# A two-layer decoder on one core: jobs of a step in a fixed order, other steps for the first cross attention's jobs, input rounding on GpSimd

## The chip, the cores and the metric

The kernel runs on one core of a Trainium2 chip. The metric is the device time of one execution in microseconds (us); the time of a kernel is the median of its runs. Engines in the profile: PE is TensorE's matmuls, PEld its weight loads, DVE is VectorE, ACT is ScalarE, POOL is GpSimd, SP is the engine that issues most DMAs.

## The reference, cut to what matters

The input `x` is 16 samples of 128 tokens by 256 features, with a context of the same shape. Two layers follow; each block adds its result to `x` and normalises the rows (mean and variance over the 256 features).

```
x = layernorm(x + ternary_attention(x))      # 2 x 256 causal, 16 heads of 16
x = layernorm(x + rope_cross(x, ctx))        # per sample, 16 heads of 8 channels, 256 x 256
x = layernorm(x + top2_of_8_experts(x))
x = layernorm(x + latent_attention(x))       # causal, 16 heads, keys from a 64-wide latent
x = layernorm(x + cross(x, ctx, ctx))        # 8 heads of 16 channels
x = layernorm(x + gated_mlp(x) + product_key_experts(x))

# every projection of the ternary attention:
sx = 127 / clip(max(abs(x), axis=-1), 1e-5);  xq = round(x * sx) / sx
y  = xq @ wq.T                               # wq in {-1, 0, 1}, scaled
```

The causal attentions work on the samples as the kernel holds them, 128 tokens by 256 features, in 16 heads.

## The kernel before

The 16 samples lie in SBUF as 16 tiles `x_t[b]` of 128 by 256. The kernel runs the ternary attention and the first cross attention in one list of beats, then the experts (rows scattered to DRAM by expert, gathered again afterwards), then the latent attention and the second cross attention in a second list of beats, then the last block.

**Beats.** `by_beats` lays out a list of blocks. A block has H beats for each sample (2 in the causal attentions, 8 in the first cross attention, 4 in the second). In beat n TensorE makes two sets of scores: those of unit n as queries by keys, whose row maxima VectorE takes (`nm`, a TENSOR_REDUCE over 128 x 1024 in PSUM tile `ps_st`), and those of unit n - lag as keys by queries, with the maxima already subtracted by a small matmul (`nmT,pick`), which ScalarE turns into exponentials (`pT`). Then come the sums of unit n - lag - 2 (`ps_o<-pT,v`, and `ps_o<-pT,ones` for the denominators). After the sums come the jobs: small pieces of work for a sample i, each with an offset, done in beat `H*i + offset` of its block.

**What fixes the order.** Inside the beats every instruction of TensorE, VectorE, ScalarE and GpSimd is kept in the order in which it is written (`tc.keep_in_program_order`). So the order of the jobs of a beat is the order on each engine. Before, the jobs of a beat stand by block, then by sample (the older sample, whose offset is larger, first), then by the block's list. In the ternary attention this gives (m is the sample whose scores are being made):

| beat | order before |
|---|---|
| even, 2m | scale_rows (m-5), out_integers (m-4), divide (m-3), maxima (m-1), project (m+1), quantise (m+2) |
| odd, 2m+1 | finish (m-4), turn (m-3), parts (m), step (m+2) |

The jobs of the ternary attention: `quantise` finds the row maxima of a sample (`am`), their scale (`isx_x`, `sx`), rounds (`qround`, `qint_x`) and makes a diagonal of the scales (`diag`, `sv`). `step` turns the integers with TensorE (`ps_m<-identb,qint_x`, copied to `qT_x` by ScalarE) and makes a row of the scales with a matmul (`ps_m<-diag,ones`). `project` makes queries, keys and values (`qk`, `v`). `parts` splits the score maxima in three bf16 parts (five small VectorE instructions that write `nmx`), `maxima` turns them (`nmT`). `divide` takes the sums by their denominators (`r` by two activations, then `oT`). `turn` turns that back to rows and rounds it like an input (`am`, `isx_o`, `sx`, `qround`, `qint_o`, from PSUM), `out_integers` turns the integers, `finish` makes the output product, adds `x` (`xn`) and takes the row statistics (`st`, `mv`, `ve`, and `rstd` on GpSimd), `scale_rows` writes `x_t[b]`.

**PSUM.** All jobs share the tiles named `ps_m`. Up to beat 45 of the first list there are three of them, used strictly in turn; from there on there is one, and the score tiles `ps_st` are three instead of two. A new tile waits until all readers of the tile that held its place are done.

**The first cross attention.** H is 8 and the lag 11. Each sample has in addition `keys` and `queries` (rotations with VectorE, ScalarE and GpSimd, and four `z` multiplications on GpSimd), `values`, `out` (ScalarE copies the sums, `ol`), `spread`, `invert` (two activations on `l`), `divide` (`l<-ol,l` on VectorE), `finish`, `scale_rows`, and the gate of the experts: `gate_turn`, and for each pair of samples, at the odd one, `gate` (logits, two exponentials), `gate_best` (top two), `gate_rows`, `places` (row numbers in the experts' buffers) and four `scatter` DMAs from GpSimd's queue.

**GpSimd's start.** Ahead of the branch that holds the attentions GpSimd clears tiles and issues the loads of the context and of the weights of the later blocks, the last being `fkeys`.

Of the kernel before, what the change touches and what calls it, by code (L numbers as in the profile page):

```python
# [14 lines left out]
ALU = mybir.AluOpType  # L15
# [8 lines left out]
ROUND = 12582912.0  # L24
# [5 lines left out]
def kernel(ctx: ExitStack, tc: tile.TileContext, a: dict, out: bass.AP):  # L30
# [17 lines left out]
    x_t = []  # L48
# [53 lines left out]
    ident = const.tile([P, P], F32, name="ident")  # L102
# [99 lines left out]
    vec, act, pool = Written(nc.vector), Written(nc.scalar), Written(nc.gpsimd)  # L202
# [35 lines left out]
    def turned(out, src, identity):  # L238
        tc.keep_in_program_order(nc.tensor.transpose(out, src, identity))
# [30 lines left out]
    def by_beats(blocks, switch=None, at=None):  # L270

        begin, beats = 0, {}
        for H, lag, score, jobs, order in blocks:
            for i, b in enumerate(order):
                for h in range(H):
                    n = begin + H * i + h  # L280
                    beats.setdefault(n, [[], [], []])[0].append((score["beat"], (b, h), 0))
                    beats.setdefault(n + lag, [[], [], []])[0].append((score["beat"], (b, h), 1))
                    beats.setdefault(n + lag + 2, [[], [], []])[1].append((score["sums"], b, h))
                for off, job in jobs:
                    if callable(off):
                        off = off(i)
                    beats.setdefault(begin + H * i + off, [[], [], []])[2].append((job, b, i))
            begin += H * len(order)
        for n in sorted(beats):
            if n == at:  # L290
                switch()
            scores, sums, jobs = beats[n]
            for f in dict.fromkeys(f for f, _, _ in scores):
                on = {which: unit for g, unit, which in scores if g is f}
                f(on.get(0), on.get(1))
            for f, b, h in sums:
                f(b, h)
            for job, b, i in jobs:
                job(b)

    def own_columns(t, hd):
# [328 lines left out]
    wmean = const.tile([P, 4], F32, name="wmean")  # L630
# [7 lines left out]
    for w in range(4):  # L638
        t = pw0.tile([P, 2, D], F32, name="wround", bufs=2)
# [42 lines left out]
    def ternary(pl):  # L682


        def quantised(src, tag):

            am = small.tile([P, 1], F32, name="am")
            vec.tensor_reduce(am, src, AX.X, ALU.max, apply_absolute_value=True)
            isx = small.tile([P, 1], F32, name=f"isx_{tag}")
            vec.tensor_scalar(isx, am, EPS, 1.0 / 127.0, ALU.max, ALU.mult)  # L690
            sx = small.tile([P, 1], F32, name="sx")
            vec.reciprocal(sx, isx)
            t = pl["w"].tile([P, D], F32, name="qround")
            vec.tensor_scalar(t, src, sx, ROUND, ALU.mult, ALU.add)
            qb = pl["w"].tile([P, D], BF16, name=f"qint_{tag}")
            vec.tensor_scalar(qb, t, ROUND, None, ALU.subtract)
            return qb, isx

        def turned_integers(qb, tag):
# [7 lines left out]
        kept = {}  # L707

        def tail(last, others):

            return lambda i: last if i >= B - 2 else others

        def quantise(b):
            qb, isx = quantised(x_t[b], "x")

            diag = pl["w"].tile([P, P], F32, name="diag")
            vec.tensor_scalar_mul(diag, ident, isx)
            sv = small.tile([P, 1], F32, name="sv")
            vec.tensor_mul(sv, isx, wmean[:, 2:3])
            kept[b] = qb, diag, sv  # L720

        def step(b):
# [42 lines left out]
        def turn(b):  # L765

            ot = pl["m"].tile([P, 2, P], F32, name="ps_m")
            for c in range(2):
                turned(ot[:, c, :], kept[b][:, c, :], ident)
            kept[b] = quantised(ot.rearrange("p c d -> p (c d)"), "o")  # L770

        def out_integers(b):
            qb, iso = kept[b]
# [13 lines left out]
        def scale_rows(b):  # L787
            xn, stats = kept.pop(b)
            scaled(x_t[b], xn, stats)

        jobs = [(6, divide), (1, parts), (2, maxima), (tail(8, 7), turn), (tail(11, 8), out_integers),
                (tail(14, 9), finish), (tail(15, 10), scale_rows), (-2, project), (-3, step), (-4, quantise)]
        return 2, 3, causal_scores(pl, kept, qk_scale), jobs, range(B)


# [91 lines left out]
    def scatter(c, n):  # L887
        pool.indirect_dma_start(
            out=xs[:, :], out_offset=bass.IndirectOffsetOnAxis(ap=place[:, c, n : n + 1], axis=0), in_=x_t[c],
            in_offset=None,  # L890
        )
# [10 lines left out]
    def rope_cross_plain(pl):  # L902

        kept = {}
# [62 lines left out]
        def scale_rows(b):  # L967
            xn, stats = kept.pop(b)
            scaled(x_t[b], xn, stats)

        jobs = [(20, out), (21, spread), (22, invert), (23, divide), (8, parts), (9, maxima), (-11, biases), (-10, keys),
                (-5, queries), (5, values), (24, finish), (25, scale_rows)]
        for beat, part in ((26, gate_turn), (28, gate), (29, gate_best), (30, gate_rows), (31, places)):
            jobs.append((beat, lambda b, part=part: part(pl, b)))

        for k in range(4):
            jobs.append((33 + 2 * k, lambda b, k=k: b % 2 and scatter(b - 1 + k // 2, k % 2)))
        return 8, 11, cross_scores(pl, 16, kept, 11), jobs, range(B)

    def rope_cross_masked(st):  # L980
# [31 lines left out]
    with tc.If(taken_out == 0) as cmp:  # L1012
        with ExitStack() as st:
            pl, switch = attention_tiles(st, 4)
            ordered[0] = True
            by_beats([ternary(pl), rope_cross_plain(pl)], switch, 2 * B + 13)
            ordered[0] = False
    with cmp.Else():
        with ExitStack() as st:
            by_beats([ternary(attention_tiles(st, 4)[0])])  # L1020
        with ExitStack() as st:
            rope_cross_masked(st)
# [126 lines left out]
    sv = early.tile([P, NR, 2, 2, 8], F32, name="sv")  # L1149
    al = early.tile([P, NR, 2, 8, 8], F32, name="al")  # L1150
    sc = early.tile([P, NR, 2, 8], F32, name="sc")
    with ExitStack() as st:
# [7 lines left out]
        kept = {}  # L1160
# [89 lines left out]
        def scale_rows(b):  # L1250
# [2 lines left out]

        latent_block = (
            2, 3, causal_scores(pl, kept),
            [(6, divide), (1, parts), (2, maxima), (7, finish), (8, scale_rows), (-2, operands), (-3, latent_keys),
             (-4, scale_latent), (-5, latent), (-6, latent_turn), (-7, scale_combined), (-8, combine),
             (lambda i: -10 - min(i, 4), fetch)], range(B),
        )
# [60 lines left out]
        def score(hf, b):  # L1320
            R = b - NR
            if R < 0:
                return
            ps = pl["m"].tile([P, 2, 64], F32, name="ps_m")
            rows = slice(hf * 64, hf * 64 + 64)
            for t in range(2):
                mm(ps[:, t, :], lhsT=routes[R][rows, t, :], rhs=fkeys[rows, t, :], start=True, stop=True)
            act.copy(rt[:, R, hf], ps)

        def best(b):  # L1330
# [10 lines left out]
            for hf in range(2):  # L1341
# [1 line left out]

        cross_block = (
            4, 6, cross_scores(pl, 8, kept1, 6),
            [(11, cross_out), (12, cross_invert), (13, cross_add), (14, cross_scale), (4, cross_parts), (5, cross_maxima),
             (0, values), (-2, queries), (18, turn_block), (19, route), (23, lambda b: score(0, b)),
             (24, lambda b: score(1, b)), (25, best)],
            [b for R in range(NR) for b in (R, NR + R)],
# [305 lines left out]
```

## Time and profile before

| | |
|---|---|
| median of 3 runs | 1509.57 us (1507.97 to 1511.66) |
| profiled execution | 1506.95 us |
| its span, first to last instruction | 1505.2 us |
| mean granted TensorE clock | 0.962 |
| PE / DVE / ACT / POOL busy | 1363.2 / 808.6 / 600.3 / 292.0 us |

Where the stages lie in the span: first scores at 27.57 us, ternary attention to about 182, first cross attention to about 535, the passage to the experts to 565, latent attention from about 893 and second cross attention from about 1040 to 1240, last block to the end.

How to read a timeline row: start in us, duration in us, engine, line of the kernel, operation, output<-inputs by the program's names, shape, count; in brackets the idle time of the engine just before it and what ended that. L195 is the helper that records VectorE, ScalarE and GpSimd instructions of the beats and L236 and L239 record TensorE's, so the rows are told apart by their tiles.

### The profile page before, as it was taken

The page shows a single profiled execution, that of the slowest core. Times are in us where ns is not written, and L with a number is a line of the kernel's source. Part 1 is how long each engine was busy: PE and PEld are TensorE (multiplying, and loading weights), DVE is VectorE, ACT ScalarE, POOL GpSimd, SP SyncE. Part 2 cuts the span into 40 slices and gives each one's busy share as a digit, 9 for nine tenths or more (in the row PEclk, how much of TensorE's full clock was granted, in tenths as well). Part 3 has the DMA queues.
Part 4 walks back from the last instruction along what each step waited for, and adds up shares of the span by engine and source line. Part 5 has one row for each costly group of instructions (what it writes and reads, how often), then busy time and mean ns, then how long its engine had stood idle before and what let it go on. Part 6 is the DMA issues. An engine that isn't in the chain of part 4 may idle for free. (4 is left out here: it accounts for less than half of the span.)

```text
span 1505.2 us, 28639 instructions
## 1 busy us (share of the span) xinstructions
PE 1363.2 (91%) x12013; PEld 860.6 (57%) x12013; DVE 808.6 (54%) x2075; ACT 600.3 (40%) x1051; POOL 292.0 (19%) x404
## 2 busy tenths in 40 slices
PE   3999899999999939999999949999999998999997
PEld 2666555555555416777777636666555544446666
DVE  6899877777777520111111047886676756543322
ACT  1544435555555522111111124554455555771110
POOL 7000233443444120000000053311122110000000
PEclk9999989999999968999999959999999998999998
DMA  9200000000000016322221041100000000000000
GB/s 309 72 2 2 2 2 2 12 12 15 12 12 15 15 35 202 98 93 93 95 92 34 20 164 33 30 2 2 2 2 2 2 2 1 1 0 12 18 7 21
DMA packets 41744, 58.16 MB, mean 39 GB/s; under 512 B 4752, under 2 KB 31392, under 8 KB 41472
## 3 DMA queue, kind: packets, MB, share of 16 engines
q1 hardware_dynamic: 35984, 41.95, 8.6%
q0 software_dynamic: 4784, 13.42, 2.7%
q8 instruction: 99, 1.62, 0.5%
q10 hardware_dynamic: 832, 0.79, 0.2%
q14 instruction: 45, 0.37, 0.1%
HBM read 39.38 MB, written 16.78 MB: 37 GB/s over the span
## 5 line engine op out<-in xcount | busy, mean ns | idle before, releaser
L195 DVE TENSOR_REDUCE nm<-ps_st 128x4 f32<-128x1024 f32 (+1 forms) x256 | 312.9, 1223 | 136.7 <-PE ps_st L236 135.3
L195 ACT ACTIVATE pT<-ps_st 128x1024 f32<-128x1024 f32 x224 | 229.4, 1024 | 206.1 <-PE ps_st L236 205.4
L195 POOL TENSOR_TENSOR rstd<-ve,nhalf 128x1 f32<-128x1 f32 x112 | 62.9, 561 | 720.0 <-DVE ve L195 555.2
L236 PE MATMUL ps_o<-pT,v 128*32 128x256 f32 (+1 forms) x2560 | 164.7, 347 | 4.2 <-ACT ol L195 3.3
L1071 DVE TENSOR_TENSOR ye<-ps_e,b 128x256 f32<-128x256 f32 x40 | 17.0, 425 | 265.1 <-PE ps_e L1068 265.1
L236 PE MATMUL ps_st<-rot,z 32*128 32x256 f32 x1024 | 147.9, 406 | 1.4 <-DVE nm L195 1.4
L1060 ACT ACTIVATE h<-ps_h,b 128x640 f32<-128x640 f32 x64 | 50.8, 794 | 228.6 <-PE ps_h L1056 228.6
L1056 PE MATMUL ps_h<-h,w 128*128 128x320 f32 x512 | 139.1, 432 | 0.0
L236 PE MATMUL ps_st<-z,rot 32*128 32x512 f32 x512 | 131.7, 592 | 0.0
L1056 PEld LDWEIGHTS ps_h<-h,w 128*128 128x128 f32 x512 | 97.3, 190 | 40.5
L236 PEld LDWEIGHTS ps_o<-pT,v 128*32 128x32 f32 x2560 | 54.8, 108 | 101.3 <-issue 81.3
L236 PE MATMUL ps_st<-nmT,pick 32*128 32x256 bf16 x1024 | 100.6, 274 | 10.3 <-ACT nmT L195 7.7
L236 PEld LDWEIGHTS ps_st<-rot,z 32*128 32x128 f32 x1024 | 90.1, 187 | 13.0 <-issue 3.4
L195 POOL DMA_INDIRECT y<-ys,place x32 | 31.1, 971 | 312.3 <-DMA ys<-ye 304.6
L236 PE MATMUL ps_o<-pT,ones 128*32 128x256 f32 x1024 | 79.4, 381 | 0.0
L236 PEld LDWEIGHTS <-pick 32*128 32x128 bf16 x1024 | 30.6, 92 | 79.6 <-issue 72.9
L1056 PE MATMUL ps_h<-xeT,w 128*128 128x320 f32 x256 | 72.9, 443 | 2.3 <-DVE xeT L1046 1.1
L236 PE MATMUL ps_st<-ctx,z 32*128 32x256 f32 x512 | 73.0, 402 | 0.0
L1068 PE MATMUL ps_e<-w,h 128*128 128x256 f32 x320 | 70.4, 379 | 0.0
L236 PE MATMUL ps_f<-fxT,fgw 128*128 128x512 f32 x128 | 62.7, 613 | 6.7 <-ACT g L1373 6.7
L236 PE MATMUL ps_st<-z,ctx 32*128 32x512 f32 x256 | 66.6, 596 | 0.0
L1068 PEld LDWEIGHTS ps_e<-w,h 128*128 128x128 f32 x320 | 60.8, 190 | 9.1
(281 smaller groups left out, 2354.8 us busy)
## 6 DMA issues: line engine op xcount, KB each, us to landing
w<-in_W_dram SPq DMA_DIRECT2D x16, 512.0 KB, 4.0
w<-in_W_dram SPq DMA_DIRECT2D x8, 1024.0 KB, 5.3
xs<-zero SPq DMA_DIRECT2D x40, 128.0 KB, 4.5
xe<-xs SPq DMA_DIRECT2D x40, 128.0 KB, 3.8
ys<-ye SPq DMA_DIRECT2D x40, 128.0 KB, 2.1
x<-in_x_dram SPq DMA_DIRECT2D x16, 128.0 KB, 6.3
ctx<-in_ctx_dram POOLq DMA_DIRECT2D x16, 128.0 KB, 5.3
out_dram<-x SPq DMA_DIRECT2D x16, 128.0 KB, 1.7
```

Source lines behind the costliest of these rows:

```text
L195: instruction = getattr(self.engine, name)(*args, **kw)
L236: tc.keep_in_program_order(nc.tensor.matmul(*args, **kw))
L1056: nc.tensor.matmul(ps[:, n, 0:H], lhsT=w[:, c, hc * P : (hc + 1) * P], rhs=src[:, c, n * H : (n + 1) * H], start=(c == 0), stop=(c == part ...
L1060: nc.scalar.activation(dst[:, hc, :].rearrange("p (n t) -> p n t", n=2), ps[:, :, 0:H], AF.Gelu, bias=b12[:, layer, e, hc : hc + 1],)
L1068: nc.tensor.matmul(ps, lhsT=h2[:, fc, c * P : (c + 1) * P], rhs=w3[:, fc, :], start=(fc == 0), stop=(fc == 3))
L1071: nc.vector.tensor_add(ye[:, c, :], ps, b3[:, e, :])
```

## The change

Three things change. First, the jobs of a beat are sorted by block, then by their place in the block's list, then by sample; and the lists are written so that `parts` and `maxima` stand first. The jobs of the ternary attention then stand so:

| beat | order after |
|---|---|
| even, 2m | maxima (m-1), divide (m-3), out_integers (m-4), scale_rows (m-5), project (m+1) |
| odd, 2m+1 | parts (m), turn (m-3), finish (m-4), step (m+2), quantise (m+3) |

Second, in the first cross attention `divide`, `finish` and `scale_rows` move two beats later, the gate's jobs two to eight beats later and the scatters eight beats later. Third, the input's `quantise` does its two rounding instructions, the diagonal and `sv` on GpSimd instead of VectorE, and stands one beat earlier (-5 for -4). `turn`, which reads PSUM, still rounds on VectorE.

```diff
@@ by_beats
-                for off, job in jobs:
+                for k, (off, job) in enumerate(jobs):
                     if callable(off):
                         off = off(i)
-                    beats.setdefault(begin + H * i + off, [[], [], []])[2].append((job, b, i))
+                    beats.setdefault(begin + H * i + off, [[], [], []])[2].append((begin, k, i, job, b))
...
-            for job, b, i in jobs:
+            for _, _, _, job, b in sorted(jobs, key=lambda j: j[:3]):
                 job(b)
@@ ternary
-        def quantised(src, tag):
+        def quantised(src, tag, eng):
...
-            vec.tensor_scalar(t, src, sx, ROUND, ALU.mult, ALU.add)
+            eng.tensor_scalar(t, src, sx, ROUND, ALU.mult, ALU.add)
             qb = pl["w"].tile([P, D], BF16, name=f"qint_{tag}")
-            vec.tensor_scalar(qb, t, ROUND, None, ALU.subtract)
+            eng.tensor_scalar(qb, t, ROUND, None, ALU.subtract)
...
-            qb, isx = quantised(x_t[b], "x")
+            qb, isx = quantised(x_t[b], "x", pool)
...
-            vec.tensor_scalar_mul(diag, ident, isx)
+            pool.tensor_scalar_mul(diag, ident, isx)
...
-            vec.tensor_mul(sv, isx, wmean[:, 2:3])
+            pool.tensor_mul(sv, isx, wmean[:, 2:3])
...
-            kept[b] = quantised(ot.rearrange("p c d -> p (c d)"), "o")
+            kept[b] = quantised(ot.rearrange("p c d -> p (c d)"), "o", vec)
...
-        jobs = [(6, divide), (1, parts), (2, maxima), (tail(8, 7), turn), (tail(11, 8), out_integers),
-                (tail(14, 9), finish), (tail(15, 10), scale_rows), (-2, project), (-3, step), (-4, quantise)]
+        jobs = [(1, parts), (2, maxima), (6, divide), (tail(8, 7), turn), (tail(11, 8), out_integers),
+                (tail(14, 9), finish), (tail(15, 10), scale_rows), (-2, project), (-3, step), (-5, quantise)]
@@ rope_cross_plain
-        jobs = [(20, out), (21, spread), (22, invert), (23, divide), (8, parts), (9, maxima), (-11, biases), (-10, keys),
-                (-5, queries), (5, values), (24, finish), (25, scale_rows)]
-        for beat, part in ((26, gate_turn), (28, gate), (29, gate_best), (30, gate_rows), (31, places)):
+        jobs = [(8, parts), (9, maxima), (20, out), (21, spread), (22, invert), (25, divide), (-11, biases), (-10, keys),
+                (-5, queries), (5, values), (26, finish), (27, scale_rows)]
+        for beat, part in ((28, gate_turn), (32, gate), (33, gate_best), (35, gate_rows), (39, places)):
...
-            jobs.append((33 + 2 * k, lambda b, k=k: b % 2 and scatter(b - 1 + k // 2, k % 2)))
+            jobs.append((41 + 2 * k, lambda b, k=k: b % 2 and scatter(b - 1 + k // 2, k % 2)))
@@ latent_block
-            [(6, divide), (1, parts), (2, maxima), (7, finish), (8, scale_rows), (-2, operands), (-3, latent_keys),
+            [(1, parts), (2, maxima), (6, divide), (7, finish), (8, scale_rows), (-2, operands), (-3, latent_keys),
@@ cross_block
-            [(11, cross_out), (12, cross_invert), (13, cross_add), (14, cross_scale), (4, cross_parts), (5, cross_maxima),
+            [(4, cross_parts), (5, cross_maxima), (11, cross_out), (12, cross_invert), (13, cross_add), (14, cross_scale),
              (0, values), (-2, queries), (18, turn_block), (19, route), (23, lambda b: score(0, b)),
```

## The prediction, made before the changed kernel was run

> **What bounds the kernel now.** I read the busy shares first, then busy times by stage, then the timelines of one period of each attention, then the waits, and last the first 40 us engine by engine.
>
> ```profile
> PE 1363.2 (91%) x12013; PEld 860.6 (57%) x12013; DVE 808.6 (54%) x2075; ACT 600.3 (40%) x1051; POOL 292.0 (19%) x404
> ```
>
> The same by stage (start:end, length, busy PE, PEld, DVE, ACT, POOL, clock):
>
> ```profile
> 60.00:148.00 88.00, 79.14 (x1265) 53.58 (x1263) 82.00 (x256) 43.43 (x85) 6.41 (x11) 1.00 0.01 2
> 212.00:535.00 323.00, 307.13 (x3290) 169.43 (x3290) 226.38 (x484) 183.86 (x284) 122.15 (x147) 1.00 0.03 12
> ```
>
> The whole says TensorE; the stages differ. In the ternary attention (60 to 148 us) VectorE is busy 82.00 of 88 and TensorE 79.14; in the first cross attention (212 to 535) TensorE is idle 323 - 307.13 = 15.9 us. VectorE in one ternary period (O: odd beat, E: even beat):
>
> ```profile
> 102.39 1.22 DVE L195 TENSOR_REDUCE nm<-ps_st 128x8 f32<-128x1024 f32 x1
> 103.52 0.48 DVE L195 SCALAR_TENSOR_TENSOR xn<-ps_m,so,x 128x256 f32<-128x256 f32 x1
> ...
> 105.62 0.48 DVE L195 TENSOR_SCALAR qround<-ps_m,sx 128x256 f32<-128x256 f32 x1
> ...
> 107.26 1.22 DVE L195 TENSOR_REDUCE nm<-ps_st 128x8 f32<-128x1024 f32 x1
> ...
> 111.95 1.22 DVE L195 TENSOR_REDUCE nm<-ps_st 128x8 f32<-128x1024 f32 x1
> ```
>
> 102.39 to 111.95 is 9.56 us, with no wait over 0.1 us: VectorE sets this period. TensorE waits in it once, for a PSUM tile:
>
> ```profile
> 152.77 0.49 PE L236 MATMUL ps_m<-diag,ones 128*128 128x128 f32 x2 [1.03 <-DVE xn L195]
> 154.97 0.45 PE L236 MATMUL ps_m<-x,xw 128*128 128x256 f32 x1 [1.71 <-DVE qround L195]
> ```
>
> `ps_m` has three tiles in rotation here. The tiles before these two are, in order, the output product (read by `xn`), the turned output (read last by `qround`), the turned integers, the row of scales. So each tile waits for the reader of the third tile before it. That rule prices the new order. The start:
>
> ```profile
> 21.27 0.35 DVE L195 TENSOR_SCALAR qround<-x,sx 128x256 f32<-128x256 f32 x1
> 22.01 0.40 PE L239 MATMUL ps_m<-identb,qint_x 128*128 128x128 bf16 x2 [2.51 <-DMA xs<-zero]
> 26.72 0.40 PE L239 MATMUL ps_m<-identb,qint_x 128*128 128x128 bf16 x2 [1.94 <-DVE qint_x L195]
> 35.21 0.61 POOL L180 DMA_DIRECT2D fkeys<-in_f_keys_dram  x1 [3.42 <-DMA b<-in_b_dram]
> 35.98 0.60 POOL L180 DMA_DIRECT2D fkeys<-in_f_keys_dram  x1 [0.16 <-issue]
> ```
>
> GpSimd issues the loads of the context and the later weights until 36.58 us. They stand ahead of the branch into the attentions, so nothing inside the branch runs on GpSimd earlier. VectorE rounds the first sample at 21.27 and TensorE starts at 22.01.
>
> **Part 1, rounding on GpSimd: the start.** `qround`, `qint_x`, `diag` and `sv` leave VectorE. On GpSimd no such operation is in the trace on these operands; the nearest is
>
> ```profile
> L195 POOL TENSOR_SCALAR z<-rot,hm 128x256 f32<-128x256 f32 x64 | 58.1, 922 | 1.6
> ```
>
> 0.92 us for the same shape, and `rstd` on 128x1 takes 0.56. I take 0.92 each for `qround` and `qint_x` and 0.56 each for the two small ones, 2.96 a sample; the lower bound is VectorE's own 0.35 + 0.29. First transpose: 36.58 + 1.84 = 38.4 instead of 22.01, 16.4 late. Two things come back: the second transpose no longer waits for VectorE behind `qk` (1.94 us; GpSimd has the second `qint_x` at 36.58 + 2.96 + 1.84 = 41.4, TensorE could take it at 38.4 + 2.8 = 41.2), so 1.8; and a wait of 0.46 for `nmx` at 37.13, since parts come first. **+14**, from +12.5 (GpSimd at VectorE's price) to +16.4 (nothing comes back).
>
> **Part 2, the ternary loop.** Off VectorE go, start to start, 0.39 + 0.21 + 0.20 + 0.07 = 0.87 a period, 9.57 to 8.7. TensorE without waits needs 9.57 - 1.03 = 8.54. But the odd beat's order is now parts, turn, finish, step: the tiles go turned output, output product, turned integers, row of scales. So the row of scales waits for `qround` of the turned output, and VectorE reaches that only after `nm`, five parts instructions and four more. From the scores ready in O: `nm` 1.26, parts 0.92 (106.34 to 107.26), `am` 0.45, `isx` 0.19, `sx` 0.20, `qround` 0.48, hand-over 0.05: 3.55. Then the row of scales to the scores of E ready, 104.05 to 106.64: 2.59. E to O, with TensorE never waiting, 106.64 to 111.00: 4.36; VectorE's and ScalarE's E work fits in it (`nmT` first, then the two for `r` end 2.3 after, `oT`, `so`, `x`, `qk` end at 4.2). GpSimd's work hides: 2.96 and the 0.56 of `rstd`, which stands ahead of it in the beat, fit in one period, and `quantise` is now two beats ahead of `step`, not one. Period 3.55 + 2.59 + 4.36 = **10.50**, longer than the 9.57 although VectorE does less. TensorE stands 1.97 us in the wait instead of 1.03. It happens where turn and step share a beat: beats 7 to 27, eleven times. Beats 9 to 27 took 60.88 to 147.87, 9.67 each, nine of them: 9 x 0.83 = 7.5; beat 7 had no finish and its period was 8.15: +2.35; in beat 27 the 1.71 wait shrinks: -0.4. **+9.4**, from -8 (no such wait: VectorE's remaining 8.77 sets the period) to +12. Queued behind the wait on TensorE are all scores of the next beat, and `nm` and `pT` wait for those.
>
> Does GpSimd slow VectorE? `x` took 0.40 us without and 0.54 with GpSimd elementwise work beside it, `qint_o` 0.29 and 0.48 (at 190.99). Only `x` lies beside the new work; 0.14 in E, where 0.1 is spare: nothing. The Trainium skill (SBUF — State Buffer, "Who interferes with whom") speaks against this move: it calls the port pair that the two engines share an exclusive lock. By that, `x` could stand a whole 0.92 us, which would add 0.8 to each of 11 periods, some 9 us; the rows show 0.14.
>
> **Part 3, the passage to the cross attention.** Waits of 0.64 (`nmx`, 176.26) and 0.59 (`oT`, 184.79) go, since parts and divide come earlier. At 197.2 the clock fell to half for 10.24 us after a wait of 1.36; VectorE's load there is the same, so I leave it. **-1**, from -6 (no half clock, 5.1 back) to +5 (twice).
>
> **Part 4, the first cross attention.**
>
> ```profile
> PE ps_m L239 <- DVE nmx L195: 9.7, 14, 0.7
> PE ps_o L236 <- ACT ol L195: 3.3, 7, 0.5
> PE ps_m L236 <- DVE l L195: 2.9, 7, 0.5
> ```
>
> These are the 15.9 us. All three causes go: parts come before `finish`'s five instructions, `out` is no longer behind the gate's exponentials, `divide` not behind `places`. But a beat has a floor: one without other TensorE work takes 2.32 (291.16 to 293.48), because its score tile is the one that `pT` is still reading. So the maxima's beat goes from 2.71 to 2.33, not to 2.04: -0.38 a sample. In odd samples the gate's beat goes 3.28 to 2.74 and finish 3.27 to 2.81, but the gate's exponentials now wait behind parts (ready 2.8 after the sums, done 3.58) and push `pT` of the next beat: 2.33 to 2.98. Odd: -0.38 - 0.54 - 0.46 + 0.65 = -0.73. A pair -1.11, 7.5 pairs: **-8.3**, from -15.9 (all of it) to -3 (even samples alone).
>
> The last scatters: those of samples 12 and 13 move behind the last `rstd`, to about 543.5, 2.67 apart (0.97 and 1.70 of wait), and are through at 551.5 to 552; the final four start at 551.98 today. **0**, at most +2.7.
>
> **Part 5, layer 1.** In the latent block only VectorE's and ScalarE's order moves; TensorE, busy 151.83 of 155, hides it: 0, and 0.35 a sample (`nmT` ahead of `r`) if it didn't. In its cross attention, five samples share a beat between `values` and the second score product, on one `ps_m` tile. Today the product goes first and `values` waits 0.36 (1121.40). Then `values` goes first and the product waits for `v`, now behind the two activations of `invert`: 1120.55 + 0.87 + 0.35 = 1121.8, product 0.65, next scores at 1122.5 instead of 1121.77: 0.72 x 5 = **+3.6**, from 0 to 5.
>
> Sum: 14 + 9.4 - 1 - 8.3 + 0 + 3.6 = **+17.7**. The profiled execution took 1506.95 (span 1505.2 and 1.75 around it), so 1524.7; the median of the runs is 2.6 above it: **1527**.
>
> **The rivals.** *The loop also loses its clock.* At 193.8 a window of 3.41 us with TensorE busy 2.06 was followed by half clock, at 1060.8 one with 1.80; at 152.8 one with 1.70 was not. A wait of 1.97 leaves 1.44. It falls whole into one such window 42 times in 100, so in some 5 of 11; each costs 1.7 (one window at half) to 5.1 (three, as at 197.2): 8 to 26 on top, about 1542. For it: fewer busy us than any window that kept its clock in a loop. Against: 152.8. The Trainium skill (TensorE: Matmul & The Clock Gate, "HAM oscillation") warns of idle gaps over about 3.4 us; by that no 2 us wait costs anything, yet 1.36 at 197.2 was enough. Chance 0.17.
>
> *The start isn't late*, the change not doing what its rows say: GpSimd reaches the rounding by 22 us or the delay is absorbed. Against it stands the 36.58. Without +14 the sum is +3.7: 1513, within 0.3% (4.5 us, about what a measurement can tell). Chance 0.08.
>
> *Faster.* VectorE's relief is the mechanism, in the loop: period 8.77 instead of 10.50, so 9 x -0.9 = -8.1, with the cross attention giving all 15.9. Then 14 - 8.1 - 1 - 15.9 + 3.6 = -7.4: 1502. It decides faster only when the period falls under 9.1 and nothing in the cross attention comes back. The tile wait at 154.97 speaks against it. Chance 0.05.
>
> **How the numbers follow.** My forecast, 1527 (own range 1518 to 1536), has 0.70. Slower: 0.70 + 0.17 = 0.87; same 0.08; faster 0.05. The range, 1514 to 1546, takes in the bounds of start and cross attention below and the half clock above.
>
> **What would show it.** Right: GpSimd's first rounding at 36.6 and the first `ps_m<-identb,qint_x` at about 38.4; `ps_m<-diag,ones` waiting about 2 us for `qround`, eleven times; periods of 10.5; no `nmx` wait after 212, the first cross attention some 8 us shorter; the wait on `rt` replaced by one on `v` near 1.1. Wrong: a loop period under 9.6, or a first transpose before 30 us.

## The result, and the profile after

The changed kernel takes 1525.31 us (median of 4 runs, 1523.77 to 1526.24), the kernel before 1508.77 us on the same chip: a ratio of 1.0105, 95% interval 1.0088 to 1.0123. It is 16.5 us slower; the forecast was 17.7 slower. The profiled execution of after took 1526.24 us with a span of 1524.5, 19.3 over the span of before, and the working below is checked against those 19.3.

I cut both traces at the same instructions and took the lengths between them (us; "maxima of sample n" is the transpose `ps_m<-identb,nmx` of that sample in the cross attention):

| stretch | before | after | difference | forecast |
|---|---|---|---|---|
| start to row of scales of sample 5 | 56.27 | 69.44 | +13.2 | +14 |
| from there to that of sample 15 (ternary loop) | 96.50 | 110.02 | +13.5 | +9.4 |
| to the cross attention's maxima of sample 1 (passage) | 68.90 | 68.84 | -0.1 | -1 |
| maxima of sample 1 to those of 15 | 293.05 | 279.88 | -13.2 | -8.3 |
| to the last rotated queries | 19.00 | 17.91 | -1.1 | in the row above |
| last rotated queries to the experts' first transposes (tail) | 31.17 | 36.10 | +4.9 | 0 to 2.7 |
| experts and latent attention, to the second cross attention | 493.60 | 493.37 | -0.2 | 0 |
| second cross attention, first to last maxima | 168.94 | 170.88 | +1.9 | +3.6 |
| the rest, to the last `ps_y` | 266.55 | 266.81 | +0.3 | 0 |

The busy times of the page hardly tell of it: VectorE lost 11 us, GpSimd gained 32.

```profile
PE 1370.0 (90%) x12013; PEld 867.4 (57%) x12013; DVE 797.5 (52%) x2011; ACT 597.5 (39%) x1051; POOL 323.8 (21%) x468
```

**The start.** First GpSimd's timeline of after, then TensorE's (start, duration, engine, line, operation; in brackets the idle time before it and what ended it):

```profile
36.22 1.35 POOL L180 DMA_DIRECT2D fkeys<-in_f_keys_dram  x2 [3.57 <-DMA b<-in_b_dram]
38.10 0.48 POOL L195 TENSOR_SCALAR qround<-x,sx 128x256 f32<-128x256 f32 x1 [0.54 <-DMA xs<-zero]
38.67 0.87 POOL L195 TENSOR_SCALAR qint_x<-qround 128x256 bf16<-128x256 f32 x1
39.53 0.61 POOL L195 TENSOR_SCALAR diag<-ident,isx_x 128x128 f32<-128x128 f32 x1
40.11 0.18 POOL L195 TENSOR_TENSOR sv<-isx_x,wmean 128x1 f32<-128x1 f32 x1
```

```profile
39.60 0.40 PE L239 MATMUL ps_m<-identb,qint_x 128*128 128x128 bf16 x2 [19.73 <-POOL qint_x L195]
```

GpSimd comes to the first rounding only after its last load, and TensorE stands 19.73 us for it: 39.60 instead of 22.01. Of these 17.6 us 4.4 come back up to the row of scales of sample 5. The wait of 1.94 us at the second transposes is gone, and TensorE is slow for a shorter time after its start: twelve matmuls that make queries and keys take 1.44 and 1.46 us for the first two samples before and 0.83 from the third on, while in after it is 1.49 for the first and 0.84 from the second on. The second sample, first before, then after:

```profile
30.57 1.46 PE L236 MATMUL ps_m<-qT_x,wqkv 128*128 128x128 bf16 x12
44.88 0.84 PE L236 MATMUL ps_m<-qT_x,wqkv 128*128 128x128 bf16 x12
```

**The ternary loop.** The same timeline of TensorE, the row of scales of successive samples:

```profile
101.50 0.46 PE L236 MATMUL ps_m<-diag,ones 128*128 128x128 f32 x2 [2.12 <-DVE qround L195]
112.18 0.46 PE L236 MATMUL ps_m<-diag,ones 128*128 128x128 f32 x2 [2.12 <-DVE qround L195]
121.28 0.46 PE L236 MATMUL ps_m<-diag,ones 128*128 128x128 f32 x2 [0.55 <-ACT qT_x L195]
131.96 0.77 PE L236 MATMUL ps_m<-diag,ones 128*128 128x128 f32 x2 [2.12 <-DVE qround L195]
144.23 0.46 PE L236 MATMUL ps_m<-diag,ones 128*128 128x128 f32 x2 [2.12 <-DVE qround L195]
```

The wait on `qround` is there, but not each time: it comes in two periods of three (10.67 us long), while in the third the row waits 0.55 us for ScalarE's `qT_x` (9.11 us). So, by these waits, the three tiles are not used strictly in turn, as the description of the kernel before and the forecast have it; why one row in three takes another tile isn't shown. Of the ten periods seven are of the long kind. The step from 131.96 to 144.23 is 12.27, and the reason is in the windows of 3.41 us around its start (busy PE, PEld, DVE, ACT, POOL, granted clock):

```profile
128.51:131.92 3.41, 1.33 (x22) 0.71 (x14) 3.10 (x11) 1.45 (x3) 0.00 (x0) 1.00 0.00 0
131.92:135.33 3.41, 3.37 (x22) 1.95 (x26) 2.02 (x8) 0.27 (x1) 1.53 (x3) 0.50 0.02 5
```

With TensorE busy for 1.33 of 3.41 us the next window runs at half clock. That happens four times in the loop of after (from 80.7, 131.9, 145.6 and 159.2), and each time the period around it is 1.6 us longer.

**The first cross attention.** All of TensorE's waits from 231 to 548 us:

```profile
PE ps_st L236 <- ACT pT L195: 0.8, 1, 0.8
```

Of 15.9 us of `nmx`, `ol` and `l` nothing is left.

**The tail.** GpSimd's scatters there:

```profile
553.02 1.30 POOL L195 DMA_INDIRECT xs<-x,place  x1 [3.25 <-DVE place L195]
557.09 0.57 POOL L195 TENSOR_TENSOR rstd<-ve,nhalf 128x1 f32<-128x1 f32 x1 [2.77 <-DVE ve L195]
...
563.27 0.96 POOL L195 DMA_INDIRECT xs<-x,place  x1 [1.72 <-DMA xs<-x,place]
567.31 0.96 POOL L195 DMA_INDIRECT xs<-x,place  x1 [3.08 <-DMA xs<-x,place]
572.16 0.96 POOL L195 DMA_INDIRECT xs<-x,place  x1 [3.89 <-DMA xs<-x,place]
```

The places of samples 14 and 15 were ready at 565.9 (19.8 us after the last rotated queries; before, 18.0), but their first scatter starts at 567.31, behind the landing of the one of sample 13, and the second waits 3.89 us for the first, where 1.70 was usual.

### The profile page after: what moved, and what is told of

Read it like the earlier page. It is cut to its first block, busy times and chain, and to the rows that moved or that the text cites. A ratio compares the mean times of both kernels' runs of the same rounds, so it can differ in the third digit from the quotient of the medians.

```text
span 1524.5 us, 28703 instructions
## 1 busy us (share of the span) xinstructions
PE 1370.0 (90%) x12013; PEld 867.4 (57%) x12013; DVE 797.5 (52%) x2011; ACT 597.5 (39%) x1051; POOL 323.8 (21%) x468
```

## Experiments on the start

Each kernel below is the changed kernel with the edit shown. The ratio is to the kernel before, measured with it.

**early_vector**: the first three samples rounded on VectorE.

```diff
-            qb, isx = quantised(x_t[b], "x", pool)
+            eng = vec if b < 3 else pool
+            qb, isx = quantised(x_t[b], "x", eng)
...
-            pool.tensor_scalar_mul(diag, ident, isx)
+            eng.tensor_scalar_mul(diag, ident, isx)
...
-            pool.tensor_mul(sv, isx, wmean[:, 2:3])
+            eng.tensor_mul(sv, isx, wmean[:, 2:3])
```

> The changed kernel with the rounding of samples 0, 1 and 2 on VectorE and that of the others on GpSimd. Theory: the first ps_m<-identb,qint_x is back at about 22.0, the start gives back its net 13 us, the loop keeps 110 us, in all about 1512 us. Rival (GpSimd, not only its start, is late): the wait comes back at sample 3, whose rounding on GpSimd is then awaited by TensorE, and less than 6 us are gained.

Measured: 1509.43 us, ratio 0.9999 (0.9986 to 1.0012). The first transposed integers are at 21.92, the row of scales of sample 5 at 54.68 instead of 69.44:

```profile
21.92 0.39 PE L239 MATMUL ps_m<-identb,qint_x 128*128 128x128 bf16 x2 [2.50 <-DMA x<-in_x_dram]
```

14.8 us come back, all of the start; the loop keeps its length but for one half-clock window (108.4, with three of them for four). Only the first samples pay for GpSimd's lateness.

**loads_sync**: the loads from `wg` to `fkeys` issued by SP, all edited like the one shown (`bg`, `b12`, `b3`, `w1q`, `w1uk`, `w1d`, `w1uv`, `w1o`, `gb`, `fq`, `fkeys`).

```diff
-    wg = load(cpool, [P, 2, 8], a["wg"].rearrange("(c p) n -> p c n", p=P), "wg", eng=nc.gpsimd)
+    wg = load(cpool, [P, 2, 8], a["wg"].rearrange("(c p) n -> p c n", p=P), "wg", eng=nc.sync)
...
```

> The changed kernel with the loads from wg to fkeys issued by SP instead of GpSimd, after its loads of x and the weights; the context's loads stay on GpSimd. Theory (GpSimd is late only by the loads that it issues ahead of the branch, of which the context's end at 25.3 us): first qround at 25.5 to 27 us and first ps_m<-identb,qint_x at 27 to 28.5 instead of 39.6, in all 10 to 12 us less, 1513 to 1515 us. Rival (something else, the branch or the clearing of xs, holds GpSimd until 36): first transposed integers stay after 36 us, no gain.

Measured: 1512.81 us, ratio 1.0017 (1.0000 to 1.0033). GpSimd's timeline now ends its loads with the context's, and goes straight on to the rounding:

```profile
23.70 1.06 POOL L44 DMA_DIRECT2D ctx<-in_ctx_dram  x2 [0.62 <-DMA ctx<-in_ctx_dram]
25.58 0.48 POOL L195 TENSOR_SCALAR qround<-x,sx 128x256 f32<-128x256 f32 x1 [0.82 <-issue]
```

TensorE starts at 27.08 and reaches sample 5's row 12.3 us earlier. What made GpSimd late were its own issues of loads, and nothing in the branch.

**round_vector**: all rounding back on VectorE, the new order kept.

```diff
-            qb, isx = quantised(x_t[b], "x", pool)
+            qb, isx = quantised(x_t[b], "x", vec)
...
-            pool.tensor_scalar_mul(diag, ident, isx)
+            vec.tensor_scalar_mul(diag, ident, isx)
...
-            pool.tensor_mul(sv, isx, wmean[:, 2:3])
+            vec.tensor_mul(sv, isx, wmean[:, 2:3])
```

> The changed kernel with the input's rounding, diagonal and sv back on VectorE, still one beat earlier. Theory (the start pays for GpSimd's late arrival, the loop pays for the tile wait whatever engine rounds): first ps_m<-identb,qint_x back at about 22.0 instead of 39.6, net 13 us back; the row of scales still waits some 2 us for qround, and the ternary loop stays at about 110 us; in all about 1512 us. Rival (the loop is longer because GpSimd works beside VectorE, the start is absorbed): the loop falls under 100 us, the start gives back under 5 us. Rival (GpSimd's share pays in the loop): VectorE's extra 0.87 a period makes the loop 118 us and the whole stays above 1520 us.

Measured: 1511.08 us, ratio 1.0003 (0.9982 to 1.0025). First transposed integers at 22.72; the loop stays at 110.4 us, and TensorE's waits over 40 to 165 us begin with

```profile
PE ps_m L236 <- DVE qround L195: 14.8, 7, 2.1
PE ps_st L236 <- DVE nm L195: 1.8, 3, 0.7
```

The first is to the tenth that of after. The wait belongs to the order of the jobs, not to the engine that rounds.

## Experiments on the ternary loop

**step_first**: one job moved in the list.

```diff
-        jobs = [(1, parts), (2, maxima), (6, divide), (tail(8, 7), turn), (tail(11, 8), out_integers),
-                (tail(14, 9), finish), (tail(15, 10), scale_rows), (-2, project), (-3, step), (-5, quantise)]
+        jobs = [(1, parts), (2, maxima), (-3, step), (6, divide), (tail(8, 7), turn), (tail(11, 8), out_integers),
+                (tail(14, 9), finish), (tail(15, 10), scale_rows), (-2, project), (-5, quantise)]
```

> The changed kernel with one job moved in the ternary list: step stands behind maxima and ahead of divide, so in the odd beat the order is parts, step, turn, finish. Theory (the row of scales waits for the tile that qround reads): it then takes a tile freed in the beat before, the seven waits of 2.1 us and the four half-clock windows behind them go, the period falls from 10.67 to 8.8 to 9.2, the ternary loop from 110.0 to 89 to 93 us, in all 1505 to 1509 us. Rival (VectorE and GpSimd side by side set the period): the row of scales no longer waits but the period stays above 10 us, in all above 1520 us.

Measured: 1505.89 us, ratio 0.9966 (0.9952 to 0.9979). The loop falls from 110.0 to 89.8 us, the period from 10.67 to 8.93, and no window in it is at half clock. TensorE's waits from 80 to 158 us, all of them:

```profile
PE ps_st L236 <- DVE nm L195: 1.9, 7, 0.4
PE ps_m L236 <- DVE bias_ov L195: 0.4, 1, 0.4
```

The row of scales of successive samples:

```profile
106.29 0.44 PE L236 MATMUL ps_m<-diag,ones 128*128 128x128 f32 x2
115.21 0.44 PE L236 MATMUL ps_m<-diag,ones 128*128 128x128 f32 x2
```

That is 20.2 us for one job's place, more than the whole change lost: even with the late start, the kernel is now 0.3% faster than before.

**step_vector**: the list of step_first, and the rounding, the diagonal and `sv` on VectorE as in round_vector. Beside the list's edit:

```diff
-            qb, isx = quantised(x_t[b], "x", pool)
+            qb, isx = quantised(x_t[b], "x", vec)
...
```

> The changed kernel with step behind maxima in the ternary list, as in step_first, and all rounding, diag and sv on VectorE. Theory (GpSimd's part pays once the tile wait is gone, because VectorE then sets the period): 0.87 us a period more on VectorE, the ternary loop from the fifth to the fifteenth row of scales 94 to 98 us where step_first had 89.8; start at 22. Rival (TensorE sets the period, the moved rounding is worth nothing): the loop stays at 89 to 91 us and the whole is 13 us below step_first, about 1493 us.

Measured: 1497.36 us, ratio 0.9924 (0.9905 to 0.9943). The loop is 99.1 us, a little above the expected 94 to 98, its period 9.93, 1.00 above step_first. From 72 to 150 us TensorE waits for the maxima again:

```profile
PE ps_st L236 <- DVE nm L195: 9.1, 7, 1.3
```

So the moved rounding is worth a full 1 us a period, once no tile wait hides it. The whole is still 0.4% below step_first, since VectorE rounds the first samples in time.

**old_order_pool**: the order of before for the ternary jobs, GpSimd's rounding from sample 3 on (as in early_vector), `quantise` at -5.

```diff
-        jobs = [(1, parts), (2, maxima), (6, divide), (tail(8, 7), turn), (tail(11, 8), out_integers),
-                (tail(14, 9), finish), (tail(15, 10), scale_rows), (-2, project), (-3, step), (-5, quantise)]
+        jobs = [(tail(15, 10), scale_rows), (tail(14, 9), finish), (tail(11, 8), out_integers), (tail(8, 7), turn),
+                (6, divide), (2, maxima), (1, parts), (-2, project), (-3, step), (-5, quantise)]
...
-            qb, isx = quantised(x_t[b], "x", pool)
+            eng = vec if b < 3 else pool
+            qb, isx = quantised(x_t[b], "x", eng)
...
```

> The changed kernel with the ternary jobs in their order of before (finish, turn, parts, step in the odd beat) and the input's rounding on GpSimd from sample 3 on, on VectorE for samples 0 to 2; quantise stays at -5. Theory (the rounding's relief counts wherever the row of scales doesn't wait for qround of the turned output, and in the old order it waits for xn, which comes before): VectorE has 0.87 less in its period of 9.57, the loop falls from 96.5 to 87 to 91 us, in all 1492 to 1496 us. Rival (the order with parts first is needed for it): the loop stays at 94 us or more, in all 1499 us or more.

Measured: 1491.22 us, ratio 0.9868 (0.9840 to 0.9896). The loop is 90.4 us, the period 8.87; the wait for `xn` that was 1.03 is now

```profile
99.00 0.46 PE L236 MATMUL ps_m<-diag,ones 128*128 128x128 f32 x2 [0.34 <-DVE xn L195]
```

**old_ternary**: the ternary part of before, the rest of after. The list of old_order_pool with `quantise` at -4, and everything of `quantise` on VectorE:

```diff
-        jobs = [(1, parts), (2, maxima), (6, divide), (tail(8, 7), turn), (tail(11, 8), out_integers),
-                (tail(14, 9), finish), (tail(15, 10), scale_rows), (-2, project), (-3, step), (-5, quantise)]
+        jobs = [(tail(15, 10), scale_rows), (tail(14, 9), finish), (tail(11, 8), out_integers), (tail(8, 7), turn),
+                (6, divide), (2, maxima), (1, parts), (-2, project), (-3, step), (-4, quantise)]
...
-            qb, isx = quantised(x_t[b], "x", pool)
+            qb, isx = quantised(x_t[b], "x", vec)
...
```

> The changed kernel with the ternary attention's jobs in their order of before, rounding on VectorE and quantise at -4: only the cross attentions' and the latent attention's edits remain. Theory (the parts of the change add up by stage): start and ternary loop as before, first cross attention 13 us shorter, its tail 5 us longer, second cross attention 2 us longer, in all 7 to 8 us below the kernel before, 1501 us. Rival (the first cross attention gained only because the ternary attention handed over in another state): its 13 us shrink to under 8, in all 1505 us or more.

Measured: 1501.05 us, ratio 0.9949 (0.9934 to 0.9965). The loop is 96.50 us as before, the first cross attention 279.6 as after. The cross attention's part of the change stands by itself.

The ordinary period (us), from the starts of `ps_m<-diag,ones`, in these kernels, without those that a half-clock window or the keys' beat lengthens:

| order of the odd beat | rounding on VectorE | on GpSimd |
|---|---|---|
| finish, turn, parts, step (before) | 9.57 | 8.87 |
| parts, turn, finish, step (after) | 10.67 to 11.57, and 9.02 in one of three | 10.67, and 9.11 in one of three |
| parts, step, turn, finish | 9.93 | 8.93 |

The rounding on GpSimd gains 0.7 or 1.0 where no tile wait stands in the way; with the order of after two periods of three are longer than before all the same. Putting `parts` first isn't needed for the gain: with the order of before the period is as short (8.87) as with `step` moved up (8.93).

## Experiments on the cross attentions

**cross_old_beats**: the beats of before for `divide` to `scatter`, `parts` and `maxima` still first.

```diff
-        jobs = [(8, parts), (9, maxima), (20, out), (21, spread), (22, invert), (25, divide), (-11, biases), (-10, keys),
-                (-5, queries), (5, values), (26, finish), (27, scale_rows)]
-        for beat, part in ((28, gate_turn), (32, gate), (33, gate_best), (35, gate_rows), (39, places)):
+        jobs = [(8, parts), (9, maxima), (20, out), (21, spread), (22, invert), (23, divide), (-11, biases), (-10, keys),
+                (-5, queries), (5, values), (24, finish), (25, scale_rows)]
+        for beat, part in ((26, gate_turn), (28, gate), (29, gate_best), (30, gate_rows), (31, places)):
...
-            jobs.append((41 + 2 * k, lambda b, k=k: b % 2 and scatter(b - 1 + k // 2, k % 2)))
+            jobs.append((33 + 2 * k, lambda b, k=k: b % 2 and scatter(b - 1 + k // 2, k % 2)))
```

> The changed kernel with the beats of before for divide, finish, scale_rows, the gate and the scatters of the first cross attention; parts and maxima still stand first in the list. Theory (each of the two edits takes away its own waits, nmx 9.7 us by the order, ol and l 6.2 us by the later beats): first cross attention, from the maxima of sample 1 to those of sample 15, 284 to 287 us, between 293 before and 280 after; its tail back to 31 us. Rival (the order alone gives it all): 280 to 281 us. Rival (the later beats give it all): 290 us or more.

Measured: 1525.26 us, ratio 1.0111 (1.0089 to 1.0133). The stretch takes 281.3 us, so the order alone gives 11.7 of the 13.2, and the later beats 1.5 on top of it; my expectation, which gave each edit its own waits, was wrong. What is left of TensorE's waits from 240 to 545 us is

```profile
PE ps_m L239 <- DVE x L195: 1.1, 5, 0.3
PE ps_m L239 <- DVE xn L195: 0.2, 1, 0.2
```

The tail is 31.8 us, 0.6 above that of before. So the later beats gained 1.5 and cost 4.3.

**tail_values**: the beats of before for the last four samples only, and `values` last in the second cross attention's list.

```diff
+        def soon(early, late):
+
+            return lambda i: early if i >= B - 4 else late
+
+        jobs = [(8, parts), (9, maxima), (20, out), (21, spread), (22, invert), (soon(23, 25), divide), (-11, biases),
+                (-10, keys), (-5, queries), (5, values), (soon(24, 26), finish), (soon(25, 27), scale_rows)]
+        for beat, part in ((soon(26, 28), gate_turn), (soon(28, 32), gate), (soon(29, 33), gate_best),
+                           (soon(30, 35), gate_rows), (soon(31, 39), places)):
...
+            jobs.append((soon(33 + 2 * k, 41 + 2 * k), lambda b, k=k: b % 2 and scatter(b - 1 + k // 2, k % 2)))
...
-             (0, values), (-2, queries), (18, turn_block), (19, route), (23, lambda b: score(0, b)),
-             (24, lambda b: score(1, b)), (25, best)],
+             (-2, queries), (18, turn_block), (19, route), (23, lambda b: score(0, b)),
+             (24, lambda b: score(1, b)), (25, best), (0, values)],
```

> The changed kernel with the beats of before for divide to scatter of the last four samples of the first cross attention only, and values last in the second cross attention's list. Theory: the tail, from the last rotated queries to the experts' first transposes, falls from 36.1 to 31 to 32.5 us; the second cross attention, from its first maxima to its last, from 170.9 to 169 us; all else stays, in all 1518 to 1520 us. Rival for the tail (the scatters' own landing, not their start, is what became late): it stays above 35 us. Rival for the second cross attention (the v wait is hidden, the difference is the clock's): it stays above 170.5 us.

Measured: 1524.95 us, ratio 1.0109 (1.0086 to 1.0133): no gain in the whole, where 5 to 7 us were expected (the profiled span, 1522.0, is 2.5 below that of after). The tail is 31.7 us, as expected, and the long periods of the second cross attention, from one `nmx<-nm` to the next, fall from 12.74 to 12.41 us. TensorE's waits from 1082 to 1215 us, of after and of this kernel, show the one wait in the other's place:

```profile
PE ps_m L236 <- ACT v L195: 3.1, 4, 0.8
```

```profile
PE ps_m L239 <- ACT rt L195: 1.8, 4, 0.4
```

But the first cross attention took 283.0 instead of 279.9, and that I had not expected. `finish` of sample 12, now early, falls in the beat of the late gate of sample 11, and both use the one `ps_m` tile:

```profile
506.71 1.13 PE L236 MATMUL ps_m<-l,xw 128*128 128x256 f32 x4
508.96 1.06 PE L236 MATMUL ps_m<-wg,gate_xT 128*128 128x8 f32 x8 [1.12 <-DVE xn L195]
```

The window from 507.6 has TensorE busy for 0.67 of it, and the next is at half clock: 1.1 of wait and, by an estimate, 1.7 of clock (half a window) make up 2.8 of the 3.1 lost.

**all_four**: the edits of early_vector, step_first and tail_values together. Their three places:

```diff
+            eng = vec if b < 3 else pool
...
+        jobs = [(1, parts), (2, maxima), (-3, step), (6, divide), (tail(8, 7), turn), (tail(11, 8), out_integers),
...
+            return lambda i: early if i >= B - 4 else late
...
```

> The changed kernel with four edits: samples 0 to 2 rounded on VectorE; step behind maxima in the ternary list; the beats of divide to scatter of before for the last four samples of the first cross attention; values last in the second cross attention's list. Theory (the changed kernel's losses are separate and add up): first transposed integers at 22, ternary loop from the fifth row of scales to the fifteenth some 90 us, first cross attention 280 us as in the changed kernel, its tail near 31.5, second cross attention near 169; in all 1485 to 1490 us. Rival (the losses share one bound, so that they overlap): above 1495 us.

Measured: 1486.15 us, ratio 0.9861 (0.9837 to 0.9885). First transposed integers at 22.21, loop 89.9, tail 31.6. The losses do add up. Against after's span of 1524.5, its 1482.5 is 42.0 less: 16.1 up to the row of scales of sample 5, 20.2 in the loop, 4.5 in the tail, 3.1 in the second cross attention (half of it by a half-clock window at its start that is missing here) and 1.3 in other stages, while the collision takes 3.1 back.

**best**: all_four without the collision.

```diff
-        jobs = [(8, parts), (9, maxima), (20, out), (21, spread), (22, invert), (soon(23, 25), divide), (-11, biases),
-                (-10, keys), (-5, queries), (5, values), (soon(24, 26), finish), (soon(25, 27), scale_rows)]
-        for beat, part in ((soon(26, 28), gate_turn), (soon(28, 32), gate), (soon(29, 33), gate_best),
-                           (soon(30, 35), gate_rows), (soon(31, 39), places)):
+        jobs = [(8, parts), (9, maxima), (20, out), (21, spread), (22, invert), (25, divide), (-11, biases), (-10, keys),
+                (-5, queries), (5, values), (26, finish), (27, scale_rows)]
+        for beat, part in ((28, gate_turn), (soon(29, 32), gate), (soon(30, 33), gate_best), (soon(31, 35), gate_rows),
+                           (soon(32, 39), places)):
...
-            jobs.append((soon(33 + 2 * k, 41 + 2 * k), lambda b, k=k: b % 2 and scatter(b - 1 + k // 2, k % 2)))
+            jobs.append((soon(34 + 2 * k, 41 + 2 * k), lambda b, k=k: b % 2 and scatter(b - 1 + k // 2, k % 2)))
```

> all_four with its first cross attention's tail done otherwise: divide, finish and scale_rows stay at the changed kernel's beats for all samples, and for the last four samples the gate's jobs follow each other at 28, 29, 30, 31, 32 and the scatters from 34. Theory (the 3.1 us that all_four and tail_values lost in the first cross attention came from finish of sample 12 and the gate of sample 11 in one beat, on one ps_m tile, and the half-clock window after it): first cross attention back to 280 us, tail 31.5 to 33.5 us, in all 1482 to 1486 us. Rival (early gates for the last samples cost the beats of the samples before, wherever they stand): first cross attention 282 us or more, no gain over 1486 us.

Measured: 1488.20 us, ratio 0.9845 (0.9821 to 0.9869). The cross attention is back at 279.9, but the tail is 34.9, beyond what was expected: the scatters of samples 12 and 13 now start right after `rstd` of sample 14, each 2.67 to 2.87 behind the last, and `rstd` of sample 15 queues behind them:

```profile
522.73 0.96 POOL L195 DMA_INDIRECT xs<-x,place  x1 [1.70 <-DMA xs<-x,place]
523.72 0.57 POOL L195 TENSOR_TENSOR rstd<-ve,nhalf 128x1 f32<-128x1 f32 x1
```

By their intervals best and all_four can't be told apart; both beat the kernel before by 1.4 to 1.5% and the changed one by some 2.5%. Nor can old_order_pool (0.9840 to 0.9896) be told from them, which leaves the ternary attention in its order of before and mends neither the tail nor the second cross attention: what the three share is the early rounding on VectorE, a row of scales that doesn't wait for `qround`, and the order in the first cross attention.

## Why the forecast was right, step by step

**The total** was right to 1.2 us (1.6 by the profiled executions: 17.7 against 19.3), its sign and its two large causes too. Three of its terms were off by 4 to 5 us each, and two of these cancel. So the sign and the causes were foreseen, but that the total came so close is in part luck.

**Start, +14, measured +13.2.** Right, shown by early_vector and loads_sync. The price of a sample was set too high (2.96 a sample; 0.48 + 0.87 + 0.61 + 0.18 = 2.14 measured: `z` was no fair row for `qround`), while the start of the first rounding was set too early (36.58, the end of the last load in the trace of before; 38.10 in that of after). The first transpose came 17.6 late, not 16.4, and 4.4 came back where 2.3 were counted: the sum left out that TensorE is slow for a shorter time after the late start. These errors cancel nearly.

**Ternary loop, +9.4, measured +13.5.** The mechanism is shown by step_first: with the row of scales ahead of `turn` the wait and 20.2 us go. Two sizes were off. The period with the wait was worked out at 10.50 and is 10.67; but it occurs in seven of the ten periods, because one row in three gets a tile that ScalarE frees, not the one that `qround` reads. And the loop does lose its clock: the rival with a chance of 0.17 was half true. Seven periods of 10.67, three of 9.11 and 1.66 for the keys' beat make 103.7; four windows at 1.6 make 110.1, and 110.02 was measured. So without the clock the term would have been +7.2. The rival's own price, 8 to 26 us, was too high: there were four such windows, not five, and each was followed by one at half clock, never three.

**Against a fast loop the forecast set the tile wait**, and this was the right thing to weigh: 8.87 to 8.93 us is what VectorE's relief gives without it, near the 8.77 of the rival called faster.

**First cross attention, -8.3, measured -13.2.** Counted from the sums of one beat to the sums of the next, the gate's beat fell from 3.28 to 2.74 and that of `finish` in odd samples from 3.3 to 2.81, as worked out. What failed is that the floor of 2.32 us holds for every beat without other TensorE work. Of the two such beats in a pair of samples, one keeps it (2.35 from 382.81 to 385.16); the other, ahead of the maxima of the samples without a gate, lasts 1.85, and the maxima's beat after it 2.28 instead of 2.33:

```profile
365.50 0.64 PE L236 MATMUL ps_o<-pT,v 128*32 128x256 f32 x8
367.35 0.64 PE L236 MATMUL ps_o<-pT,v 128*32 128x256 f32 x8
369.63 0.64 PE L236 MATMUL ps_o<-pT,v 128*32 128x256 f32 x8
...
387.90 0.64 PE L236 MATMUL ps_o<-pT,v 128*32 128x256 f32 x8
390.69 0.64 PE L236 MATMUL ps_o<-pT,v 128*32 128x256 f32 x8
```

The last two rows are the maxima's beat behind the gate. It is longer, as the forecast has it, but by less: 2.67 to 2.85 us in this stretch against 2.23 to 2.28 without a gate, where 2.98 was worked out. The two together are 0.65 to 0.85 a pair: a pair went from 42.5 to 40.6 us, -1.9 and not -1.11. Why just that one beat falls under the floor isn't settled.

**Tail, 0 to +2.7, measured +4.9.** The step looked only at when the last four scatters can be issued. It left out that the places of the last pair come 1.8 later, and that the waits between scatters are not always 1.70: 3.08 and 3.89 here. cross_old_beats shows that it is the later beats that cost it. The other kernels agree: with the later beats for all samples the tail is 33.4 us (loads_sync) to 36.2, with those of before for the last four 31.6 to 31.8. Why these two landed late isn't settled.

**Second cross attention, +3.6, measured +1.9.** The wait on `v` is there in the place of that on `rt`, but 0.8 instead of the 1.1 worked out: 12.74 less 12.32 is 0.42 for each of the long periods, not 0.72. tail_values gives 0.33 of it back by the order of the list alone.

**Passage, -1, measured -0.1.** The waits on `nmx` (1.1 us) did go and that on `oT` fell from 0.59 to 0.23, but the waits of TensorE for `nm` grew from 1.4 to 2.4 us. A window busy for 0.49 of it at 220.7 us is followed by 10.24 us at half clock, as one at 193.8 was before.

## What to carry to other kernels

When jobs are reordered on a shared set of tiles, price each new tile by the last reader of the tile whose place it takes, and look where that reader now stands in its engine's queue; one job moved was worth 20 us here, more than the work taken off the busiest engine. GpSimd, which issues loads at the start, was late here for its first arithmetic by the length of its issues, so give the first items of a loop to another engine. And moving jobs to later beats gained a little inside the loop here (1.5 us) and was paid at its end (4.3), where no other work covers it.

## What the runs showed of the hardware

**Windows and the clock.** In the ternary loops of the six kernels with the `qround` wait, windows of 3.41 us with TensorE busy up to 0.46 of it were followed by half clock, those with 0.48 or more kept theirs, and 0.47 went either way; no wait in these loops was over 2.12 us. In the first cross attention of tail_values a window with 0.67 lost it, so the busy share alone doesn't decide. The Trainium skill (TensorE: Matmul & The Clock Gate, "HAM oscillation") puts the limit at idle gaps of more than about 3.4 us; these runs show that shorter ones are enough.

**GpSimd beside VectorE.** GpSimd's prices for the moved instructions, from 60 to 148 us of after (busy time and mean ns behind the bar):

```profile
L195 POOL TENSOR_SCALAR qint_x<-qround 128x256 bf16<-128x256 f32 x9 | 7.8, 864 | 0.8
L195 POOL TENSOR_SCALAR diag<-ident,isx_x 128x128 f32<-128x128 f32 x9 | 5.6, 618 | 0.0
L195 POOL TENSOR_SCALAR qround<-x,sx 128x256 f32<-128x256 f32 x9 | 4.3, 479 | 13.5 <-PE ps_o L236 7.3 <-PE ps_st L236 4.6 <-POOL rstd L195 1.2
```

On VectorE the three took 294, 281 and 353 ns before. VectorE's own instructions beside them were hardly slowed. In the loop of after only two of nine `x` lie beside a GpSimd instruction (423 and 431 ns, against the 404 of before); in that of step_first all nine do (least, median, most):

```profile
L195 DVE TENSOR_SCALAR x<-xn,mv,rstd x9: 402/404/503, 85.9 to 158.6; 128x256 f32<-128x256 f32 x9
```

In old_order_pool all nine do too, eight at 403 to 406 ns and one at 620. By the exclusive lock of the Trainium skill (SBUF — State Buffer, "Who interferes with whom") the forecast had put some 9 us on this at most; these two loops show a lengthening of 0.1 and 0.2 us in one of nine.
